# Key and value chunks of a second attention layer moved to the end of a mixture, shorter second tiles, and other loads at the joins, in a two-layer gated Flamingo kernel

## The chip, the cores and the metric

The kernel runs on one NeuronCore of a Trainium2 chip. The metric is the device time of one execution in microseconds (us); lower is better. All arithmetic is in float32; a float32 product shows as two records on TensorE. Engines are named as in the profile: PE is TensorE's matmul, PEld its weight load, DVE VectorE, ACT ScalarE, POOL GpSimd, SP SyncE; PEq, SPq and so on are their sequencers.

## The reference

`x` is 8 x 100 x 512, the context 8 x 722 x 512 with a boolean mask. Four gated steps are added to `x` in turn:

```
x = x + tanh(g_xattn[0]) * L0_xattn(context, layernorm(x), mask)   # 16 heads of 64; queries of x, keys and values of context and x
x = x + tanh(g_ffn[0])   * L0_ffn(layernorm(x))                    # 4 experts, F = 2048, top 2
x = x + tanh(g_xattn[1]) * L1_xattn(layernorm(x), context)         # 16 heads of 32; every 16th context row per head
x = x + tanh(g_ffn[1])   * L1_ffn(layernorm(x))                    # 8 experts, F = 1024, top 2

xattn 0: kv = concat(layernorm(context), layernorm(x)) @ Wkv;  softmax(q k^T, masked) v @ Wout, then layernorm
ffn:     h = silu(x @ w1[e]) * (x @ w3[e]);  out = sum over the 2 chosen experts of gate * (h @ w2[e])
xattn 1: K, V = context @ Wk.T + bk, context @ Wv.T + bv, head h takes rows h, h + 16, h + 32, ...
```

The mask leaves few context rows in use, so that layer 0 works on the gathered valid rows.

## The kernel before, in words

**Prologue.** SP loads the inputs; the masks are scanned into running counts, which POOL writes to DRAM (`cum_d`, L273) and SP broadcasts to all partitions into a part of `wo` (L274 to L277), with half of layer 0's value weights (`wv`) loaded before and after. `few` (L277) is read by every engine, and the branch at L1261 chooses between `attend_to_all` (L631) and `attend_to_few` (L893). The trace takes the second.

**Layer 0's attention** (`attend_to_few`) works on four pairs of batch rows (`Pair`, L942). `find` (L911) turns counts into row numbers, `fetch` (L958) gathers context rows (`ct`). `softmax` (L1074) handles one chunk of two heads for both rows: scores on PE (`ps_sf`), a biased maximum on DVE (L1093), exponentials on ACT (L1103), reciprocal and product on DVE (L1107, L1108). `weigh` (L1113) transposes (`ps_tl`, `ps_tc`) and multiplies by the values (`po_f`). A pair has eight chunks; between them a list `fill` (L1181 to L1257) of steps with costs is worked off in proportion: the next pair's projections, the output projections of the pair before (`project_pair`, L311, its products called `py_w`), and the routing of its rows (`norm_rows`, `route`). The costs only set the place of a step. The fill of the last pair is the output projection and the routing of blocks 4 and 5, the search for the first slot of mixture 0 (`first0.find`, L488 to L565, by generator pieces: DVE's sums, counts `pp_f` on PE, `place` at L541, `pe_f` at L549, then the rows), and two of the four chunks of layer 1's keys and values (`keys_values_1`, L571: per chunk four steps of 16 records; `k1T` and `v1T` written by ACT at L594). The output projection of block 6 is split in two and laid around the last chunk (`project_parts`, L295).

**Mixtures.** `Mixture.run` (L1544) computes slots: up to 256 rows of one expert. `xt` rows are gathered by POOL from the normed rows `xnd` (`fetch`, L1521), transposed (L1563) and copied (`xTs`, L1566), then `pa` and `pb` (L1617), gate (L1625 to L1627) and `py_e` (L1589 or L1600), and added to the accumulator by a scattered DMA (L1659). The first slot of 256 is chosen before all rows are known: from row blocks up to `EARLY0` (6) or `EARLY1`; the rest is planned by `dispatch` (L1281) while it runs. Mixture 0 has a first slot of 256, two of 192 and four of 256; mixture 1 a first of 256, four of 160, three of 128 and two of 256. A slot of 192 or 160 gathers and transposes two tiles of 128 rows, of which the second is used by 64 or 32 rows. `ahead` steps of the deferred work (`late`: project, route) run before the first slot's transposes, the others between its matmuls. Before mixture 0 that is one step, the projection of block 7 (`last_outputs`, L1775). The pools of the attention are released before it, and tiles of the mixture lie where they were.

**Between the mixtures.** `ending` (L1787) loads eight pieces and one weight tile and runs chunks 2 and 3 of layer 1's keys and values (`pkv`, L584) behind the last slot's last product. Then come the row loads (L1809), `normed` (L1824: statistics on DVE, root on POOL, transposes `pt_x`, copies `xT` on ACT), `queries_1` (L1842, `pq`), `set_apart` (L1857, `apartv` on ACT, `apartk` on POOL), `scores_1` and so on, and in the last row blocks the search for mixture 1's first slot (`first1.find`) and the routing. Weights of that slot are loaded early with `begin_weights` (L1539): `w1(0)`, `w3(0)` after the expert is known, `w2(0)` when the index copy `e_late` is written, which is ordered behind the row numbers (L563, L564).

Of the kernel before, what the change touches and what calls it, by code (L numbers as in the profile page):

```python
# [8 lines left out]
FP = mybir.dt.float32  # L9
# [4 lines left out]
ALU = mybir.AluOpType  # L14
# [50 lines left out]
def flamingo_gated(  # L65
# [86 lines left out]
    def load_kv0(pool, tag, i, bufs=1):  # L152

        t = pool.tile([P, KC, 512], FP, tag=tag, name="wkv", bufs=bufs)
        nc.sync.dma_start(t, wkv_r[:, :, bass.ts(i, 512)])
        return t
# [101 lines left out]
    with ExitStack() as ph:  # L258
# [12 lines left out]

        cum0 = wo.rearrange("p c n -> p (c n)")[:, : 2 * CTX]
        wv = [load_kv0(wpool, "wv0", 2)]  # L273
        nc.sync.dma_start(cum0, cum_d[0].partition_broadcast(P))  # L274
        wv.append(load_kv0(wpool, "wv1", 3))
# [19 lines left out]
    def project_parts(b, cuts, ps, tag, work, y_tag="y", y_bufs=1):  # L295

        n = IN0 // P
        py = ps.tile([P, 512], FP, tag=tag, name="py")
        for c in range(n):
            if c in cuts:  # L300
                yield
            nc.tensor.matmul(
                py[:S], oT0[:, c, bass.ts(b % 2, S)], wo[:, c, :], start=(c == 0), stop=(c == n - 1)
            )
        add_normed(b, py, work, y_tag, y_bufs)

    def project_out(b, *where):
        for _ in project_parts(b, (), *where):
            pass
# [165 lines left out]
    class First:  # L475
# [12 lines left out]
        def find(self, space, ps, tag):  # L488
# [58 lines left out]
            for t in range(2):  # L547
                for k in range(b):
                    self.counted = nc.tensor.matmul(  # L549
                        pe[:, bass.ts(t, 2)], place[:, k, bass.ts(t, P)], what[:, k],  # L550
                        start=(k == 0), stop=(k == b - 1),
                    )
# [7 lines left out]
            known = v.scalar_tensor_tensor(  # L560
                self.rows, both[:, :, 0], -1.0, free, ALU.add, ALU.add
            )
            with tc.issue_after(known.ins):  # L563
                v.tensor_copy(self.e_late, number)  # L564
# [43 lines left out]
    def half_square(t, src, h):  # L608
        nc.sync.dma_start(t, src[:, bass.ts(h, D // 2)].rearrange("(c p) n -> p c n", p=P))
        return t  # L610

    def load_heads():
# [4 lines left out]
        def load(c, kc):  # L617
            if kc < 2:
                t = wv[kc]
# [11 lines left out]
    def attend_to_all():  # L631
# [209 lines left out]

        load_x(2, 3)
        wk = [load_kv0(kvp, "wk", i, 2) for i in range(2)]
# [3 lines left out]
        for b in range(B):  # L847
# [24 lines left out]
            if b <= EARLY0:  # L872
                project_out(b, ps_mm, "mm", work, "o", 2)
            if b < EARLY0:
# [4 lines left out]
        for _, step in keys_values_1(  # L879
            (0, 1),  # L880
            lambda: [
                half_square(
                    kvp.tile([P, KC, 512], FP, tag="wk", name="wkv1", bufs=2)[:, :, : D // 2], w, 0
                )
                for w in (wk1, wv1)
            ],
            load_heads(),
# [5 lines left out]
    def attend_to_few():  # L893
# [264 lines left out]
        find(0, cum0)  # L1158
        pair.fetch()
        wk = [load_kv0(kvp, "wk", i, 2) for i in range(2)]  # L1160
# [3 lines left out]
        for k, (_, step) in enumerate(pair.steps()):  # L1164
# [6 lines left out]
            (0, 1),  # L1171
            lambda: [
                half_square(
                    kvp.tile([P, KC, 512], FP, tag="wk", name="wkv1")[:, :, : D // 2], w, 0
                )
                for w in (wk1, wv1)
            ],
            load_heads(),
# [3 lines left out]
        for i in range(PAIRS):  # L1182
# [11 lines left out]
            else:  # L1194
# [3 lines left out]
                c = (0.5, lambda: next(choice, None))  # L1198
                norms, routes = routes
                fill = fill + norms[:1] + kv[:2] + routes[:1] + norms[1:] + kv[2:3] + routes[1:]  # L1200
                fill += [c, kv[3], kv[4], c, c, kv[5], c, kv[6], c, kv[7], c]
# [19 lines left out]
            for c in range(n):  # L1221
                now = softmax(pair, c)
                if following is None and c == n - 1:

                    parts = project_parts(EARLY0, (3, n - 2), ps_mm, "mm", work)
                    fill.insert(-1, (0, lambda: next(parts)))
                while done < len(fill) and (cost < whole * (c + 1) / n or c == n - 1):
# [6 lines left out]
            if following is None:  # L1234
                next(parts)
                finish(*last)
                next(parts, None)
                for _ in choice:
                    pass
                break  # L1240
            finish(*last)
# [258 lines left out]
    class Mixture:  # L1500
# [20 lines left out]
        def fetch(self, rows, k0, T, upto=B):  # L1521

            xts = []
            for k in range(k0, k0 + (T + P - 1) // P):
                xt = ein.tile([P, D], FP, tag="xt", name="xt", bufs=4)
# [4 lines left out]
                    in_offset=bass.IndirectOffsetOnAxis(ap=rows[:, k : k + 1], axis=0),  # L1530
# [13 lines left out]
        def run(self, before, late, ahead, pace, between=None, ending=None):  # L1544
# [13 lines left out]
            def transposed(xts):  # L1558
                xT = ein.tile([P, KC, WHOLE], FP, tag="xTs", name="xTs", bufs=2)
                for t, xt in enumerate(xts):  # L1560
                    pt = ps.tile([P, 512], FP, tag="m", name="pt_s")
                    for kc in range(KC):
                        nc.tensor.transpose(  # L1563
                            pt[:, bass.ts(kc, P)], xt[:, bass.ts(kc, P)], ident
                        )
                    nc.vector.tensor_copy(  # L1566
                        xT[:, :, bass.ts(t, P)], pt.rearrange("p (k s) -> p k s", s=P)
# [133 lines left out]
            def ready():  # L1701
# [3 lines left out]

            xT = slot(
                self.e, self.w0, WHOLE, transposed(self.xts), first.rows, first.gate, 0,
# [67 lines left out]
    def last_outputs(ps, work):  # L1775
        for b in range(EARLY0 + 1, B):
# [10 lines left out]
    def ending(ps):  # L1787

        pieces = [(c, kc) for c in (2, 3) for kc in range(KC)]
        tiles = {}  # L1790
        for c, kc in pieces[:3]:
            t = spaces["heads"].tile([P, 4 * B * M1], FP, name=f"ch{c}{kc}")
            tiles[c, kc] = heads_into(t, c, kc)
        w = wts.tile([P, KC, 512], FP, tag="w1", name="wkv1", bufs=3)
        w = [half_square(w[:, :, bass.ts(i, D // 2)], m, 1) for i, m in enumerate((wk1, wv1))]
        for (c, kc), tag in zip(pieces[3:], ("w3", "w2", "w1", "w3", "w2")):
# [287 lines left out]
```

## Time and profile before

| what | value |
|---|---|
| median of three runs | 1432.19 us (1431.19 to 1440.32) |
| profiled execution: run, span | 1431.09 us, 1429.4 us |
| mean granted PE clock | 0.986 |
| layer 0's attention | about 16 to 409 us |
| mixture 0: first `pa` to last `py_e` | 415.39 to 971.84 us |
| layer 1's attention | about 985 to 1098 us |
| mixture 1: first `pa` to its last `py_e` | 1101.56 to 1413 us |

The profile gives for each engine its busy time and, for idle time in front of an instruction, what ended it. A row of the timeline has start, length, engine, line, operation, output and inputs, count and, in brackets, idle time and its releaser. Waits of a queue's own (SPq) are time in which SP could issue no transfer. The chain of waits follows the last instruction back through its releasers; a row with DMA means that a transfer was what was waited for. The granted clock is 1.00 at full speed; a stretch at half speed shows the same matmuls with double distance from start to start.

### The profile page before, as it was taken

The numbers are of one execution on the slowest core, as the hardware profiler recorded it, in microseconds if no ns is written. First come the engines' busy times: TensorE is split into PE (matmuls) and PEld (weight loads), VectorE is DVE, ScalarE is ACT, GpSimd is POOL, SyncE is SP. The second block draws the span as 40 slices with busy tenths as digits, with TensorE's granted clock in tenths as the row PEclk, the third lists the DMA queues.
The fourth block names the chain that finished last, engine by engine and source line by source line (L and its number), as shares of the span: only waits on it lengthen the run. The fifth ranks groups of instructions, "written<-read, shape, count | busy, mean of one in ns | idle before, by whom it ended". The sixth has DMA issues, their size and how long they took to land. (4 is left out here: it accounts for less than half of the span.)

```text
span 1429.4 us, 18472 instructions
## 1 busy us (share of the span) xinstructions
PE 1362.0 (95%) x7181; PEld 1027.8 (72%) x7181; DVE 485.8 (34%) x1405; ACT 252.3 (18%) x729; POOL 189.4 (13%) x279
## 2 busy tenths in 40 slices
PE   4999999999979999999999999998998999999995
PEld 4566756767557789997777776773666789988773
DVE  4353644535735221212121211113374623223220
ACT  1124423334311000100000000002452101101000
POOL 3410211100130110000010000003321111111000
PEclk9999999999999999999999999998998999999998
DMA  8300101111367365664364535513016478779521
GB/s 296 107 1 0 41 7 34 60 30 48 107 256 293 140 206 214 223 229 135 134 206 167 168 121 190 170 63 84 13 47 226 177 254 284 244 243 344 201 45 17
DMA packets 103892, 208.13 MB, mean 146 GB/s; under 512 B 6198, under 2 KB 13370, under 8 KB 103780
## 3 DMA queue, kind: packets, MB, share of 16 engines
q1 hardware_dynamic: 95556, 186.72, 36.7%
q0 software_dynamic: 8224, 19.97, 5.8%
q8 instruction: 63, 1.03, 0.3%
q14 instruction: 49, 0.40, 0.1%
HBM read 191.45 MB, written 15.23 MB: 145 GB/s over the span
## 5 line engine op out<-in xcount | busy, mean ns | idle before, releaser
L1617 PE MATMUL pa<-xTs,w 128*128 128x256 f32 (+3 forms) x1536 | 314.5, 347 | 1.6 <-DVE xTs L1566 1.6
L1617 PE MATMUL pb<-xTs,w 128*128 128x256 f32 (+3 forms) x1536 | 309.8, 344 | 0.0
L1617 PEld LDWEIGHTS pa<-xTs,w 128*128 128x128 f32 x1536 | 260.2, 191 | 32.7 <-issue 8.9
L1617 PEld LDWEIGHTS pb<-xTs,w 128*128 128x128 f32 x1536 | 260.9, 191 | 21.7
L1600 PE MATMUL py_e<-w,hT 128*128 128x512 f32 x464 | 204.4, 592 | 0.0
L1625 ACT ACTIVATE sg<-pa 128x256 f32<-128x256 f32 (+3 forms) x192 | 66.9, 349 | 692.5 <-PE pa L1617 680.1
L1626 DVE TENSOR_TENSOR sg<-sg,pa 128x256 f32<-128x256 f32 (+3 forms) x192 | 72.3, 377 | 341.9 <-ACT sg L1625 338.8
L1600 PEld LDWEIGHTS py_e<-w,hT 128*128 128x128 f32 x464 | 87.1, 190 | 97.0 <-issue 94.7
L1627 DVE TENSOR_TENSOR hT<-sg,pb 128x256 f32<-128x256 f32 (+3 forms) x192 | 72.3, 377 | 121.2 <-PE pb L1617 119.6
L1065 PE MATMUL pv_f<-wkv,kvT 128*100 128x512 f32 (+1 forms) x192 | 86.2, 597 | 0.0
L1589 PE MATMUL py_e<-hT,w 128*128 128x192 f32 (+1 forms) x512 | 79.0, 313 | 0.0
L1589 PEld LDWEIGHTS py_e<-hT,w 128*128 128x128 f32 x512 | 76.8, 190 | 0.0
L1526 POOL DMA_INDIRECT xt<-xnd,rows x27 | 26.6, 986 | 368.9 <-PE pt_s L1563 277.4
L1051 PE MATMUL pk_f<-kvT,wkv 128*128 128x328 f32 x256 | 73.3, 443 | 1.1 <-ACT kvT L1022 1.0
L1103 ACT ACTIVATE pr_f<-pr_f,nmax 100x228 f32<-100x228 f32 x128 | 60.7, 475 | 35.6 <-DVE nmax L1093 33.4
L1051 PEld LDWEIGHTS pk_f<-kvT,wkv 128*128 128x128 f32 x256 | 47.8, 190 | 24.0 <-ACT kvT L1022 2.1
L1065 PEld LDWEIGHTS pv_f<-wkv,kvT 128*100 128x100 f32 (+1 forms) x192 | 32.6, 174 | 44.1 <-issue 42.0
L1093 DVE CUSTOM_DVE_ANT_0 pr_f<-ps_sf,bias 100x228 f32<-100x228 f32 x128 | 43.7, 391 | 54.5 <-PE ps_sf L1080 54.3
L1659 POOL DMA_INDIRECT xr<-ye,rows x12 | 18.7, 1558 | 267.5 <-DVE ye L1658 266.9
L1035 PE MATMUL pq_f<-kvT,wq 128*128 128x200 f32 x256 | 47.4, 346 | 6.7 <-ACT kvT L1022 3.9
L1035 PEld LDWEIGHTS pq_f<-kvT,wq 128*128 128x128 f32 x256 | 45.4, 198 | 8.0 <-ACT kvT L1022 4.6
L1566 DVE COPY xTs<-pt_s 128x512 f32<-128x512 f32 x31 | 20.3, 687 | 84.9 <-PE pt_s L1563 81.6
(379 smaller groups left out, 1217.9 us busy)
## 6 DMA issues: line engine op xcount, KB each, us to landing
w<-in_f_w_dram SPq DMA_DIRECT2D x144, 1024.0 KB
ch<-in_ctx_heads_dram SPq DMA_DIRECT2D x8, 720.0 KB
wkv<-in_wkv_dram SPq DMA_DIRECT2D x4, 1024.0 KB
wq<-in_ctx_heads_dram SPq DMA_DIRECT2D x4, 720.0 KB
wkv<-in_ctx_heads_dram SPq DMA_DIRECT2D x4, 720.0 KB
kT<-cum_d SPq DMA_DIRECT2D x3, 722.0 KB
wq<-in_wq_dram SPq DMA_DIRECT2D x4, 512.0 KB
wo<-in_wo_dram SPq DMA_DIRECT2D x1, 2048.0 KB
```

The source lines that it names most:

```text
L1035: nc.tensor.matmul(pq[:, bass.ts(i, 2 * S)].rearrange("p (j s) -> p j s", j=2), wq[:, kc, bass.ts(c0 + i, P)], self.lats[kc], start=(kc == 0),
L1051: nc.tensor.matmul(pk[:, : S + FK], wk[c // 4][:, kc, bass.ts(c % 4, P)], self.kvT[:, kc], start=(kc == 0), stop=(kc == KC - 1),)
L1065: nc.tensor.matmul(pv[:n], self.kvT[:, kc, k0 : k0 + n], wv[hf][:, kc, :], start=(kc == 0), stop=(kc == KC - 1),)
L1093: nc.vector.tensor_tensor_reduce(out=pr[:, r, j], in0=ps[:S, r, bass.ts(j, FK)], in1=p.bias[j], scale=-1.0, scalar=FMAX, op0=ALU.add, op1= ...
L1103: nc.scalar.activation(pr[:, r, j], pr[:, r, j], AF.Exp, bias=nmax, scale=-1.0, accum_out=sm[:, r, j : j + 1],)
L1526: nc.gpsimd.indirect_dma_start(out=xt, out_offset=None, in_=xnd[: LEAD + upto * S], in_offset=bass.IndirectOffsetOnAxis(ap=rows[:, k : k + ...
L1589: nc.tensor.matmul(pys[c // 2][:, bass.ts(c % 2, T)], w2[:, i, bass.ts(c, P)], hT[:, i, :T], start=False, stop=(fg == F // FG - 1 and i == ...
L1600: nc.tensor.matmul(py[:n], hT[:, i, c : c + n], w2[:, i, :], start=(fg == 0 and i == 0), stop=(fg == F // FG - 1 and i == FG // P - 1),)
L1617: nc.tensor.matmul(p[:, :T], w[:, kc, bass.ts(i, P)], xT[:, kc, :T], start=(kc == 0), stop=(kc == KC - 1),)
L1625: nc.scalar.activation(sg[:, :T], pa[:, :T], AF.Sigmoid)
L1626: nc.vector.tensor_tensor(sg[:, :T], sg[:, :T], pa[:, :T], ALU.mult)
L1627: nc.vector.tensor_tensor(hT[:, i, :T], sg[:, :T], pb[:, :T], ALU.mult)
```

## The change

Chunk 0 of layer 1's keys and values stays in the last pair; chunks 1, 2 and 3 are computed in `ending`, with 12 pieces instead of eight and the weights in two tiles of 384 columns. Piece 10 and 11 take the places of piece 0 and 1 after the steps that read those. Block 6's output projection is no longer laid around the last chunk; it and block 7's run ahead of the first slot's transposes (`ahead` 2). `find`'s last piece stands directly before the release of the attention's pools. The value weights `wv` and the counts are loaded after the branch, the counts first and into the space of a key weight tile. The second tiles of slots of 192 and 160 are gathered and transposed by their 64 or 32 rows. In layer 1's last row blocks, the ordering of the routing behind `pe_f` is gone, and `w2(0)` of mixture 1 is asked for after the first slot's transposed rows are copied. The core of the diff:

```diff
-        cum0 = wo.rearrange("p c n -> p (c n)")[:, : 2 * CTX]
-        wv = [load_kv0(wpool, "wv0", 2)]
-        nc.sync.dma_start(cum0, cum_d[0].partition_broadcast(P))
-        wv.append(load_kv0(wpool, "wv1", 3))
...
-        find(0, cum0)
+        wk, wv = kv0_tiles(kvp, "wk"), kv0_tiles(kvp, "wv")
+
+        space = bring(0, wk[0])
+        load_kv0(wv, 2)
+        find(0, space)
         pair.fetch()
-        wk = [load_kv0(kvp, "wk", i, 2) for i in range(2)]
+        load_kv0(wk, 0)
         load_x(2, 3)
         load_rest()
...
-            (0, 1),
+            (0,),
             lambda: [
-                half_square(
-                    kvp.tile([P, KC, 512], FP, tag="wk", name="wkv1")[:, :, : D // 2], w, 0
-                )
+                chunks_of(kvp.tile([P, KC, 512], FP, tag="wk", name="wkv1"), w, 0, 1)
...
-                c = (0.5, lambda: next(choice, None))
+                c = (0.2, lambda: next(choice, None))
                 norms, routes = routes
-                fill = fill + norms[:1] + kv[:2] + routes[:1] + norms[1:] + kv[2:3] + routes[1:]
-                fill += [c, kv[3], kv[4], c, c, kv[5], c, kv[6], c, kv[7], c]
+                fill = fill + norms[:1] + routes[:1] + norms[1:] + routes[1:]
+                fill += [c, kv[0], c, c, kv[1], c, kv[2], c]
...
-                if following is None and c == n - 1:
-
-                    parts = project_parts(EARLY0, (3, n - 2), ps_mm, "mm", work)
-                    fill.insert(-1, (0, lambda: next(parts)))
-                while done < len(fill) and (cost < whole * (c + 1) / n or c == n - 1):
+                while done < len(fill) and cost < whole * (c + 1) / n:
...
             if following is None:
-                next(parts)
-                finish(*last)
-                next(parts, None)
+                kv[3][1]()
+            finish(*last)
+            if following is None:
                 for _ in choice:
                     pass
-                break
-            finish(*last)
...
-                xt = ein.tile([P, D], FP, tag="xt", name="xt", bufs=4)
+                n = min(P, T - (k - k0) * P)
+                xt = ein.tile([P, D], FP, tag="xt", name="xt", bufs=4)[:n]
...
+            xT = transposed(self.xts)
+            if len(self.w0) < 3:
+
+                with tc.issue_after(self.copied.ins):
+                    nc.vector.tensor_copy(first.e_late, first.e)
+                self.begin_weights()
...
-        for b in range(EARLY0 + 1, B):
+        for b in range(EARLY0, B):
...
+        for i in range(3):
+            head_piece(i, i)
+        w = [
+            chunks_of(wts.tile([P, KC, 512], FP, tag="w1", name="wkv1", bufs=3), m, 1, 3)
+            for m in (wk1, wv1)
+        ]
+        for i, tag in enumerate(("w1", "w3", "w2", "w3", "w2", "w3")):
+            piece(3 + i, tag)
         yield
+        piece(9, "w2")
...
+        for i, (_, step) in enumerate(steps):
             step()
-
-    mix.run(last_outputs, range(EARLY0, B), 1, 1, between, ending)
+            if i < 2:
+                head_piece(10 + i, i)
+
+    mix.run(last_outputs, range(EARLY0, B), 2, 1, between, ending)
...
-            if b > EARLY1 + 1:
-                xn = norm_rows(b - 1, wk_, out, nc.sync)
-            elif b:
-                logits = route(b - 1, *how)
+            if b:
+                logits = route(
+                    b - 1, ps_t, "t", wk_, wg, lg1, out, nc.scalar.copy, nc.sync
+                )
...
-                with tc.issue_after(first1.counted.ins):
-                    logits = route(b - 1, *how, xn)
-                    project_1(b, oT)
-            else:
-                project_1(b, oT)
+            project_1(b, oT)
...
-        mix.begin_weights()
```

## The prediction

> **What bounds the kernel now.** I read the page's first part, then the busy time by stretch, then, for each stretch in which PE is not full, PE's timeline with what released it, the queue's own waits and the chain. Times are us from the span's start.
>
> ```profile
> PE 1362.0 (95%) x7181; PEld 1027.8 (72%) x7181; DVE 485.8 (34%) x1405; ACT 252.3 (18%) x729; POOL 189.4 (13%) x279
> ```
>
> PE is the bound and nothing else is near. A change can remove PE work, remove PE's idle time, or alter the clock at which PE runs. By stretch (columns: length, then PE, PEld, DVE, ACT, POOL busy, granted clock, DMA share, GB/s):
>
> ```profile
> 341.00:416.00 75.00, 66.28 (x479) 37.84 (x479) 44.69 (x158) 22.57 (x75) 14.61 (x24) 0.98 0.29 104
> 416.00:971.80 555.80, 555.74 (x2496) 442.73 (x2494) 125.92 (x367) 47.68 (x122) 35.57 (x32) 1.00 0.52 182
> 971.80:1001.00 29.20, 22.38 (x170) 11.45 (x170) 10.69 (x25) 8.42 (x19) 12.38 (x27) 0.82 0.31 76
> 1086.00:1101.60 15.60, 13.05 (x49) 8.64 (x49) 4.11 (x12) 0.66 (x2) 3.46 (x5) 0.67 0.92 334
> 1101.60:1413.00 311.40, 311.36 (x1828) 262.47 (x1828) 94.60 (x303) 32.04 (x90) 40.66 (x34) 1.00 0.62 213
> ```
>
> Both mixtures are full. What can be won lies at three joins: into mixture 0, out of it, into mixture 1. The first, on PE's timeline:
>
> ```profile
> 401.74 7.08 PE L302 MATMUL py<-wo,oT 128*100 128x512 f32 x16 [1.88 <-DVE y L362]
> 412.07 0.63 PE L1563 MATMUL pt_s<-ident,xt 128*128 128x128 f32 x4 [3.25 <-issue]
> 413.48 1.12 PE L1563 MATMUL pt_s<-ident,xt 128*128 128x128 f32 x4 [0.78 <-DVE xTs L1566]
> 415.39 1.22 PE L1617 MATMUL pa<-xTs,w 128*128 128x256 f32 x2 [0.80 <-DVE xTs L1566]
> ```
>
> PE waits for the gathered rows. Their numbers were known at 394.7, but POOL and SP stood until row block 6's output norm had left the released pool (DVE L366, done 403.56):
>
> ```profile
> SPq L1276 <- DVE x L366: 14.1, 1, 14.1
> ```
>
> So the gathers went out at 404.43 and 405.84, and the second landed at 412.82. The second join, PE, then ACT:
>
> ```profile
> 971.84 9.89 PE L584 MATMUL pkv<-ch,wkv 128*32 128x360 f32 x128
> 985.42 0.53 PE L1833 MATMUL pt_x<-ident,xn 100*128 100x100 f32 x4 [3.70 <-ACT apartv L1867]
> 991.81 5.60 PE L1845 MATMUL pq<-xT,wq 128*128 128x400 f32 x8 [0.58 <-ACT xT L1836]
> 997.60 2.88 PE L1845 MATMUL pq<-xT,wq 128*128 128x400 f32 x8
> ```
> ```profile
> 983.57 2.90 ACT L1867 COPY apartv<-v1T 32x180 f32<-32x180 f32 x8 [1.22 <-POOL mv L239]
> 986.50 0.49 ACT L1836 COPY xT<-pt_x 128x400 f32<-128x400 f32 x1
> ```
>
> The same eight pq records take 5.60 and 2.88: half clock. The third join is on the chain of waits:
>
> ```profile
> 1084.25 7.26 DMA w<-in_f_w_dram
> 1091.51 1.09 POOL xt L1526
> 1092.91 7.17 DMA xt<-xnd,f_rows
> 1101.56 1.99 PE pa L1617 x8
> ```
>
> **The change part by part.** The sum goes against this execution: span 1429.4, run 1431.09, 1.1 under the median 1432.19.
>
> *1. Prologue.* SP no longer loads wv and the broadcast of the counts before the branch; both follow it. The counts (L274) were issued at 13.29 and landed at 17.67, 4.4 later; issued at 16.1 they land near 20.5, and DVE's search L918 starts there instead of 19.40 (DVE passes its branch only at 19.17): ct's gather is up to 1.1 later. Against that, DVE now takes the first qT copy ahead of ct's statistics, so the last queries no longer wait (2.79 idle before 33.10); values then wait for the second qT copy, which still stands behind ct's normalization (34.64 + 0.57), and start at about 35.3 instead of 35.91. I take -0.6. Bounds: -2 (two thirds of the 2.79) to +3 (SP's branch takes 4.0, as at 965.45, instead of the 0.5 seen at 15.6, and all behind it follows). SP's order after the branch (counts, wv, keys, x, wo) is 2.7 MB ahead of the keys; at the 390 GB/s of these slices this is 7 us, landing near 24, before values ask.
>
> *2. Last pair and first join.* From 340.95 to pa at 415.39 are 74.4; PE's idle times over 0.25 in it add to 8.6, so 65.8 is work. One chunk leaves: four steps at 1.25 to 1.35, 5.2. Row block 6's projection (16 records, 6.9) stays on PE but goes behind the search. Work after: 60.6. Both fillers covered softmax chains of this pair: from the end of a chunk's scores to its transposes are 3.95 (four reduces 1.35, exponentials 1.9 starting 0.45 after the first, reciprocal 0.18, product 1.1). Laying the new order by hand with these rows (scores 1.0, transposes 0.8, weighing 0.85, py_w 5.5), I find stalls of 0.55 before the weighing of chunk 0, 1.85 before block 4's router rows, 1.6 before the search's counts, 0.95 before the weighing of chunk 7, and 3.25 for the search's DVE steps before pe_f: 8.2. The first three would be longer by what DVE has queued. pe_f then ends near 391.4 to 394, against 394.1. Behind it the loads of w (3 MB) and both gathers go out at once, at 392 to 395, since block 6 and 7 no longer lie before the release. Blocks 6 and 7 then hold PE for 13.75, longer than the gather's 7.2, so the 3.25 wait goes; left are two xTs copies, about 2.3. Stalls 10.5 + 60.6 give pa at 412.0; the durations alone, laid end to end, give 409.1, but the same laying puts before's pa 2.6 too early. I take 411, -4.5. Bounds: 409.1 with full clock at pa (before loses 3.3 there: 256-wide records 0.43 apart instead of 0.216 until 420.25), about -10; and half clock over py, below, +9.
>
> *3. Clock at this join.* It was full over py after a gap of 1.88 and half after the three waits that add to 4.8 out of 7 us. After, 5.8 of the 10 us ahead of pe_f are idle, so the half clock probably moves to py, for the 6.7 to 10 us that it lasted at the joins: 3.3 to 5.0 lost there, 3.3 saved at pa. Net 0. Bounds inside the former.
> The Trainium skill, "TensorE: Matmul & The Clock Gate", Part 1, puts half rate behind an idle window of about 3.4 us and full rate after about 3.4 us of steady work. The row differs: at the third join a gap of 1.77 was followed by half clock for 10 us. By the page an estimate of py's loss is 1.7 at most, and the sum would be 1.6 lower, at 1422; the row's longer loss speaks against the change where the page's shorter one speaks for it.
>
> *4. Second join.* Three chunks at the end instead of two: 4.95 more PE (9.89 for two), ending at 986.7. SP's eight early pieces (720 KB each) and two weight loads now stand before mixture 0's last branch, and pieces 9 to 11 behind it; the last waits for step 1 (about 974.5). With the branch of 4.0 the first row block's load goes at about 980.2 instead of 978.88, and DVE and POOL follow by 1.3; this alone gives pq at 993.1. ACT is later still: k1T and v1T to 987.9, 1.2 branch, eight copies 2.9, four xT copies 0.5 each from 992.05: pq at 994.2, +2.4. The chunk's 4.95 is thus half hidden by the wait that was 3.70 and the four short ones. Bounds: +1 (row chain alone) to +7 (load issued at 986, behind the pieces). The clock's loss of 2.7 I leave; gone, the part is -0.3.
>
> *5. Third join.* The copy of e_late, w2(0) and the next group's weights now wait for the transposed rows. So the gathers no longer fly beside 4 MB: 7.17 from issue to landing becomes nearer 3.35 (ct's gather at 59.49, landed 62.84, with the queue quiet): -3.8. Block 6's router rows now come before pe_f and fill part of the 1.77 but wait for xn (1087.4): pe_f ends 0.5 earlier, and 0.8 is lost elsewhere. I take -3.5. Bounds: 0 (gather as slow as 7.17) to -5. The late weights are 4 MB, 10.5 us at 400 GB/s; the first is asked for 13.8 and w2(0) 27 after pa starts, so they are hidden; without cover, 1:1.
>
> *6. Rows alone.* In mixture 0 two second tiles of 64 rows, in mixture 1 four of 32. A full tile's four transposes hold PE for 0.435 (0.87 for two tiles); those of 100 rows stand 0.085 apart against 0.109. In proportion to rows a tile of 64 saves 0.2 and one of 32 saves 0.28, 1.5 together; I take -1.2. Bounds: 0 (copies and transposes cost the same) to -2.6 (all six tiles free). The copies are off the path:
>
> ```profile
> L1566 DVE COPY xTs<-pt_s 128x512 f32<-128x512 f32 x31 | 20.3, 687 | 84.9 <-PE pt_s L1563 81.6 <-DMA w<-in_f_w_dram 3.1
> L1563 PE MATMUL pt_s<-ident,xt 128*128 128x128 f32 x124 | 17.3, 279 | 5.6 <-issue 3.2 <-DMA xt<-xnd,f_rows 1.3 <-DVE xTs L1566 0.8
> ```
>
> *Sum.* -0.6 - 4.5 + 0 + 2.4 - 3.5 - 1.2 = -7.4: 1423.7, and 1424 as a forecast of the median.
>
> **The rivals.** *A, slower: the half clock covers all of py.* Place: blocks 6 and 7, 13.75 of work after 10 us of which 5.8 are idle. At half rate all of it costs 13.75 more: 1424 + 13.75 = 1438. Above 7.4 us of py work at half rate the whole change loses. For it: third join, where 1.77 was enough and the clock stayed low for 10. Against it: no stretch of half clock in this trace lasts over 10 us, which costs 5 and gives 1429 less what pa saves.
> *B: SP's queue decides the second join.* Pieces 10 and 11 stand before the row loads, and if the branch or a slot holds SP until 986, pq comes 12.9 later (978.88 to 991.81), at 999: +7 instead of +2.4, 1429; up to 1434 if the scatter's 4.7 us landing (972.97 to 977.7) is also slowed by the extra 2 MB. Against: the pieces' slots are free early by PE's order.
> *C: nothing visible.* The chunk is paid out in one place and in at another (-5.2 and +4.95), the gather was as slow beside out's write as beside w, and only part 6 remains: 1430.
> *D: every join gains.* Part 1 at -2, part 2 at -10, part 4 at -0.3, part 5 at -5, part 6 at -2.6 is -20: 1411; half of that beyond the sum gives 1414 as its middle. For it: clock lost now is 3.3 + 2.7 + 2.2 at the joins. Against: the last pair has less to fill with.
>
> **How the numbers follow.** Forecast 0.50 (own range 1418 to 1430), A 0.10, B 0.13, C 0.10, D 0.17. The range 1412 to 1438 leaves out the lower half of D, the upper of A and a little that I have not thought of, about 0.17. One per cent is 14.3, about what a measurement of this kernel tells from no change: faster, below 1417.9, has most of D and 0.06 of the forecast, 0.22; slower, above 1446.5, has only unnamed cases and A with B, 0.06; the rest, 0.72, is within.
>
> **What would show it.** Right: pa of mixture 0 near 411 with py ending near 406 and no DMA wait before pt_s; pkv with 192 records ending 14.8 after the last down; pq 2 to 3 later after that down than the 20 of before; at the third join xt landing within 4 of its issue and no w in flight. Wrong: the last pair's stalls over 12; py at 1.7 per pair; xs loads issued after 982; a wait of pa on w in mixture 1's second group, 14 us after its start.

## The result, and the profile after

The changed kernel takes 1436.16 us (median of 12 runs, 1432.65 to 1441.16) against 1433.08 for the kernel before beside it (12 runs, 1428.33 to 1440.32): a ratio of 1.0032, 95% interval 1.0017 to 1.0048. It is slower, by 3.1 us between the two medians and by about 4.6 us by the ratio, 0.2 to 0.3%; the forecast was 1424, a gain. The profiled execution ran 1436.99 us with a span of 1435.3 and a mean clock of 0.979.

Cutting both traces at the same events shows where the two profiled executions differ. Each row is the time between the starts of two kinds of work on PE, in us:

| stretch | before | after | difference |
|---|---|---|---|
| start to the last pair's first `py_w` | 335.34 | 335.09 | -0.25 |
| that to mixture 0's first `pa` | 80.05 | 83.19 | +3.14 |
| mixture 0, to the last `pkv` chunks' start | 556.45 | 554.32 | -2.13 |
| `pkv` start to the first `pq` | 19.97 | 24.40 | +4.43 |
| first to last `pq` | 27.57 | 26.73 | -0.84 |
| last `pq` to mixture 1's first `pa` | 82.18 | 81.82 | -0.36 |
| mixture 1, to PE's last record | 311.75 | 313.85 | +2.10 |

A `pkv` start is also the end of mixture 0's last product, called the last down below.

The page's first part, and the busy time by stretch of the changed kernel (columns as before):

```profile
PE 1368.0 (95%) x7181; PEld 1034.4 (72%) x7181; DVE 482.8 (34%) x1404; ACT 252.2 (18%) x729; POOL 187.8 (13%) x279
```
```profile
341.00:418.20 77.20, 64.94 (x412) 40.59 (x408) 42.84 (x156) 21.52 (x73) 14.97 (x25) 0.87 0.27 97
418.20:972.60 554.40, 554.26 (x2496) 441.36 (x2496) 125.81 (x369) 47.57 (x122) 35.52 (x32) 1.00 0.51 179
972.60:1006.00 33.40, 27.36 (x236) 13.88 (x236) 10.77 (x25) 10.02 (x22) 12.18 (x27) 0.85 0.44 134
1082.00:1105.50 23.50, 19.41 (x100) 11.91 (x96) 12.14 (x46) 2.84 (x9) 6.18 (x8) 0.80 0.41 144
```

PE has as many records as before and is busy 6 us longer. Much of the same work took longer: the granted clock of the last pair and first join fell from 0.98 to 0.87. PE's timeline there:

```profile
366.92 0.93 PE L381 MATMUL pt_r<-ident,xn 100*128 100x100 f32 x4 [2.14 <-DVE xn L245]
367.77 1.84 PE L1071 MATMUL ps_sf<-kT,qT 64*100 64x228 f32 x6
393.08 5.22 PE L543 MATMUL pe_f<-space 100*128 100x2 f32 x24 [3.18 <-DVE space L535]
398.76 16.23 PE L296 MATMUL py<-wo,oT 128*100 128x512 f32 x32 [0.46 <-DVE space L551]
414.82 0.60 PE L1552 MATMUL pt_s<-ident,xt 128*128 128x128 f32 x4
418.28 1.99 PE L1607 MATMUL pa<-xTs,w 128*128 128x256 f32 x8 [1.26 <-DVE xTs L1555]
```

The gathered rows no longer hold PE, as forecast. But the six score records take 1.84 where the same six took 1.01 before, `pe_f` 5.22 instead of 2.74, and the 32 records of blocks 6 and 7 take 16.23 where two times 6.9 were counted. The clock's record in the trace has two half-rate stretches here, 365.8 to 376.0 and 393.1 to 403.4; before it had none in the pair and one at 413.5 to 420.3, in front of `pa`.

The second join, PE, ACT and SP's own waits:

```profile
972.60 14.73 PE L574 MATMUL pkv<-ch,wkv 128*32 128x360 f32 x192
990.90 0.90 PE L1842 MATMUL pt_x<-ident,xn 100*128 100x100 f32 x4 [3.57 <-PEq L1744]
997.00 4.76 PE L1854 MATMUL pq<-xT,wq 128*128 128x400 f32 x8 [0.58 <-ACT xT L1845]
```
```profile
989.25 2.90 ACT L1876 COPY apartv<-v1T 32x180 f32<-32x180 f32 x8 [1.30 <-DMA x<-xr]
992.17 0.49 ACT L1845 COPY xT<-pt_x 128x400 f32<-128x400 f32 x1
```
```profile
SPq L1744 <- SPq L1744: 8.3, 3, 5.5
SPq L1818 <- DMA xr<-ye,rows: 0.2, 1, 0.2
```

ACT is where the forecast put it (first xT copy forecast at 992.05, seen at 992.17). The rows are not: their first load went at 984.81, 12.2 after the last down, where it was 7.0 before. SP was held behind its branch until 0.2 before that, and the scattered rows finished at the same moment (4.7 us after issue before, 9.9 now).

The third join, from the chain of waits:

```profile
1095.38 2.17 PE pe_f L543 x20
1098.41 1.10 POOL xt L1514
1099.82 3.78 DMA xt<-xnd,f_rows
1105.56 3.78 PE pa L1607 x8
```

The gather's flight fell from 7.17 to 3.78, as forecast. But `pe_f` ended 2.6 later after the last `pq` than before. The projections in front of it ran at half clock (1082.6 to 1089.4), and four projection records (1.96) that stood behind it before now run ahead of it; together this took more than the wait of 1.77 that is gone and the full clock of `pe_f` itself (2.17 for 4.39) gave back. And `pa`, 1.99 for eight records before, started at half clock.

### The profile page after: what moved, and what is told of

Its sections match the earlier page's. It is cut to its first block, busy times and chain, and to the rows that moved or that the text cites. A ratio compares the mean times of both kernels' runs of the same rounds, so it can differ in the third digit from the quotient of the medians.

```text
span 1435.3 us, 18479 instructions
## 1 busy us (share of the span) xinstructions
PE 1368.0 (95%) x7181; PEld 1034.4 (72%) x7181; DVE 482.8 (34%) x1404; ACT 252.2 (18%) x729; POOL 187.8 (13%) x279
## 5 line engine op out<-in xcount | busy, mean ns | idle before, releaser
L1555 DVE COPY xTs<-pt_s 128x512 f32<-128x512 f32 (+2 forms) x31 | 18.1, 618 | 83.1 <-PE pt_s L1552 83.1
```

## The experiments

All stretches below are read from one profiled execution each, in the cuts of the table: P for the last pair and first join (80.05 before, 83.19 changed), J for `pkv` to `pq` (19.97, 24.40), T for last `pq` to mixture 1's `pa` (82.18, 81.82).

**e1, two chunks in the pair again.**

```diff
-            (0,),
+            (0, 1),
...
-                fill = fill + norms[:1] + routes[:1] + norms[1:] + routes[1:]
-                fill += [c, kv[0], c, c, kv[1], c, kv[2], c]
+                fill = fill + norms[:1] + kv[:2] + routes[:1] + norms[1:] + kv[2:3] + routes[1:]
+                fill += [c, kv[3], kv[4], c, c, kv[5], c, kv[6], c]
...
-        chunks = (1, 2, 3)
+        chunks = (2, 3)
```

> The changed kernel with chunks 0 and 1 in the last pair again and 2 and 3 at the end; all else as changed. Theory T (clock and SP's queue): the emptied last pair fell to half clock from 367 to 377, and SP's late pieces held the row loads. Then the first loss and the second join's go: the stretch 367 to 377 is at full clock, mixture 0's first pa starts at 412 to 415 instead of 418.3, and from the last down's end to pq it is 20 again instead of 24.4; 5 to 9 us below the changed kernel, so about 1428 where that is 1436. Rival R1 (the chunk is only shifted, and the loss lies in the order of the joins): pa later by 5 of the chunk, the end earlier by 5, and within 1.5 us of the changed kernel.

1434.05 us, ratio to before 1.0001 (0.9979 to 1.0024): by the two ratios 4.4 below the changed kernel, not the 5 to 9 expected. The end behaved as expected: J is 18.95, and the row loads go 7.03 after the last down. The pair did not: P is 87.31, 4.1 more than the changed kernel, with half clock at 378.4 to 388.7 and 398.9 to 409.1. The chunk alone does not keep the pair full. Block 6's projection, 6.9 of work, is missing there too. So the theory had to be widened to all the work taken out of the pair.

**e2, the wait ahead of `pe_f` filled.**

```diff
+                t = ps_mm.tile([P, 512], FP, tag="mm", name="warm")
+                for k in range(4):
+                    nc.tensor.matmul(
+                        t[:S], oT0[:, k % 8, bass.ts(0, S)], wo[:, k % 8, :],
+                        start=True, stop=True,
+                    )
                 for _ in choice:
                     pass
```

> The changed kernel with four extra products of the output projection (512 columns each, 0.86 us each at full clock, results unused) ahead of pe_f, three of them in the wait of 3.2 us there. Theory T: it is the wait that drops the clock; with it filled, pe_f takes 2.7 instead of 5.2 and the 16 py products 13.75 instead of 16.2, and mixture 0's first pa comes about 4 earlier (5 less some 0.9 for the fourth product). Rival R2 (the half clock comes from the whole thin stretch from 356 on, in which PE idles and transposes, or from no fixed cause): pe_f and py stay at 5.2 and 16.2 and pa is 0 to 1 later.

1435.53 us, 1.0015 (0.9994 to 1.0035). P is 79.85, 3.3 less (about 4 were expected), although work was added. PE's timeline:

```profile
390.92 2.82 PE L1229 MATMUL warm<-wo,oT 128*100 128x512 f32 x6
394.01 2.81 PE L543 MATMUL pe_f<-space 100*128 100x2 f32 x24 [0.27 <-DVE space L535]
397.28 15.60 PE L296 MATMUL py<-wo,oT 128*100 128x512 f32 x32 [0.46 <-DVE space L551]
416.18 1.99 PE L1613 MATMUL pa<-xTs,w 128*128 128x256 f32 x8 [1.25 <-DVE xTs L1561]
```

`pe_f` is at full speed again. The second stretch of half clock shrank from 10.2 to 3.4 us (397.2 to 400.6) but did not go; the first, at 366.5, is untouched, as nothing was put there. So the wait ahead of `pe_f` was paid twice in the changed kernel: as a wait, and as half clock behind it.

**e3, the last two pieces from ACT's queue; e4, without them; e10, without the last three.** The diffs of e3 and e10 (e4 is the second part of e10's alone). In e4 and e10 the steps of the pieces that are left out multiply pieces already there:

```diff
-                head_piece(10 + i, i)
+                head_piece(10 + i, i, nc.scalar)
```
```diff
-        piece(9, "w2")
+        tiles[pieces[9]] = tiles[pieces[3]]
...
-                head_piece(10 + i, i)
+                tiles[pieces[10 + i]] = tiles[pieces[i]]
```

> The changed kernel with the last two pieces of the heads (10 and 11) issued by ACT's queue instead of SP's; the same bytes at the same time. Theory T-queue (SP stands before them, and its branch of 5.5 us comes after): SP passes the branch some 4 us earlier; if that alone held the row loads they go at 979 to 981 instead of 984.8 and pq comes 2.5 earlier (then ACT's copies end last). Theory T-scatter (the pieces' bytes delay the scattered rows, landing 9.9 after issue instead of 4.7): row loads stay at about 984.8 behind the scatter, and the time is that of the changed kernel.

> The changed kernel without loading pieces 10 and 11: steps 10 and 11 multiply pieces 0 and 1 again, so part of chunk 3's keys and values is wrong by intention and its load is left out. Both forms of theory T: row loads go at 979 to 980.5 and the scattered rows land about 5 after their issue; pq then waits for ACT's copies and comes at 994 to 995 instead of 997.0, 2 to 3 us less in all. Rival R1 (the second join is late only since PE ends 5 later): pq stays at 997.

> The changed kernel without loading pieces 9, 10 and 11: their steps multiply pieces 3, 0 and 1, so part of chunk 3's keys and values is not computed from its own data, the routing behind it differs, and only the second join is read. Theory T-scatter: with no piece behind the last slot, the last scatter lands 4.7 after its issue as before (9.9 changed, 7.0 without the last two), the row loads go 7.1 to 8 after the last down (12.2 changed), and pq waits for ACT's copies alone: 22 to 22.6 after the last down, the +2.4 of the forecast. Rival: landing stays above 6.5 or pq at 24.

e3: 1438.41 us, 1.0042 (1.0017 to 1.0067), not better. SP reaches its branch 2.6 earlier after the last down (0.5 against 3.1), yet J is 24.61. e4's time (1489.8) is that of another routing, with one more slot behind mixture 1, and says nothing; e10's one time likewise. Their second joins, side by side:

| | scatter, issue to end | SP, branch to first wait for rows | row load after last down | J |
|---|---|---|---|---|
| before | 4.7 | 6.6 | 7.0 | 19.97 |
| changed | 9.9 | 9.0 | 12.2 | 24.40 |
| e3 | 10.1 | 11.4 | 12.4 | 24.61 |
| e4 | 7.0 | 6.9 | 9.3 | 22.83 |
| e10 | 4.7 | 5.3 | 7.1 | 22.30 |

SP's waits in e10, in the stretch of that join:

```profile
SPq L1818 <- DMA xr<-ye,rows: 8.1, 1, 8.1
SPq L595 <- PE py_e L1590: 6.5, 1, 6.5
SPq L1744 <- SPq L1744: 4.6, 1, 4.6
```

With the bytes gone SP is through its branch early and waits 8.1 for the scatter, as before's 6.8; `pq` then waits for ACT alone, at +2.3 where 2.4 was forecast. With the bytes there, issued by whom ever, the scatter takes 5.2 longer than before and SP's way 2.4 (changed) or 4.8 (e3) longer, and SP then waits only 0.2 or 0.5 for the scatter. The trace tells what SP does on that way. From the branch to its first semaphore wait are 4.0 us before, 5.6 in the changed kernel and 5.1 in e3; behind that, in the changed kernel and e3, it waits for the landing of the pieces, also of those that ACT issued: until 983.79 for the piece that landed at 983.78 in the changed kernel, until 977.33, 980.05 and 982.75 in e3, where the three pieces landed at 977.31, 980.04 and 982.74. So it is the pieces' 2.2 MB in flight that count, whichever queue issues them: they slow the scatter, and SP waits for them as well. In all five the scatter is what SP waited for last; in the changed kernel and e3 a faster scatter alone would have gained no more than the 0.2 or 0.5. The one piece left in e4 costs the scatter 2.3, the two further ones 2.9.

**e5, pair and end as before; e6, only the split projection back; e7, all the pair's waits filled.** e5 takes the pair's code, `project_parts` and `ending` from the kernel before; its core is the first diff. e6 and e7 are shown against the changed kernel; e7 has e2's four products ahead of `pe_f` as well:

```diff
-                fill = fill + norms[:1] + routes[:1] + norms[1:] + routes[1:]
-                fill += [c, kv[0], c, c, kv[1], c, kv[2], c]
+                fill = fill + norms[:1] + kv[:2] + routes[:1] + norms[1:] + kv[2:3] + routes[1:]
+                fill += [c, kv[3], kv[4], c, c, kv[5], c, kv[6], c, kv[7], c]
...
-        chunks = (1, 2, 3)
+        chunks = (2, 3)
...
-    mix.run(last_outputs, range(EARLY0, B), 2, 1, between, ending)
+    mix.run(last_outputs, range(EARLY0, B), 1, 1, between, ending)
```

```diff
-                fill = fill + norms[:1] + routes[:1] + norms[1:] + routes[1:]
-                fill += [c, kv[0], c, c, kv[1], c, kv[2], c]
+                fill = fill + norms[:1] + kv[:1] + routes[:1] + norms[1:] + kv[1:2] + routes[1:]
+                fill += [c, kv[2], c, c, kv[3], c, c, c]
...
+                    parts = project_parts(EARLY0, (3, n - 2), ps_mm, "mm", work)
+                    fill.insert(-1, (0, lambda: next(parts)))
```

```diff
+                def more():
+                    t = ps_mm.tile([P, 512], FP, tag="mm", name="warm")
+                    for k in range(2):
+                        nc.tensor.matmul(
+                            t[:S], wo[:, k, : S], wo[:, k, :], start=True, stop=True
+                        )
...
+                fill = fill + norms[:1] + w + w + routes[:1] + norms[1:] + w + routes[1:]
```

> The changed kernel with the last pair, block 6's split projection and the end of mixture 0 as before (two chunks in the pair, two at the end); what stays of the change are the prologue, the second tiles by rows alone and the third join. Theory T: both losses sit in what is undone here, so the last pair runs at full clock and mixture 0's first pa follows the pair's first output products by 80 as before (83.2 changed), pq follows the last down by 20 (24.4 changed), and the gain of the third join and of the rows stays: 3 to 5 below the kernel before, about 1427 where before is 1431.5. Rival R3 (the loss sits in the third join or the prologue): not faster than before.

> The changed kernel with block 6's projection split around the last chunk again and the one chunk's steps spread early in the pair; three chunks still at the end. Theory T as sharpened by the first runs (it is all the work taken out of the pair, chunk and projection, that leaves PE thin enough for the half clock): with the projection's 6.9 back in the pair, one of the two stretches of half clock goes, and pa follows the pair's first output products by 75 to 79 instead of 83.2 (5 below the 80 of before is the chunk, if no clock is lost). Rival R4 (the chunk alone decides): both stretches stay and it is 82 or more. The second join stays late, 24 from last down to pq.

> The changed kernel with extra products (512 columns, results unused) in the pair's waits: six early in the pair beside the four ahead of pe_f. Theory T: no stretch of half clock between 340 and 420; py and pe_f at full clock, and although 5 to 8 us of useless work is added, pa follows the pair's first output products by 78 to 82 instead of 83.2. Rival R2 (no link between filled waits and clock): half clock stays and pa is later by the added work, 86 to 90.

e5: 1432.97 us, 1.0011 (0.9996 to 1.0026). Both losses are gone (P 79.61, J 19.79) and T is 80.03, 2.2 less than before; but mixture 1 takes 313.44 against 311.75, because the half clock now lies in its first slot. It does not beat the kernel before: this expectation failed in its last step. e6: 1434.82, 1.0023 (1.0002 to 1.0044); P is 80.90, between the two expectations, with 10.2 us of half clock at 378.5 and two stretches of 3.4. e7: 1432.97, 1.0006 (0.9988 to 1.0025); half clock between 340 and 420 falls from 20.5 us to 10.2, where none was expected, and P is 79.52: 3.7 shorter than the changed kernel with ten useless products of 0.86 more. The busy time by stretch, changed and then e7:

```profile
355.00:366.00 11.00, 6.25 (x62) 4.12 (x60) 10.45 (x32) 6.17 (x23) 3.20 (x8) 0.99 0.08 23
366.00:377.00 11.00, 10.09 (x52) 6.45 (x52) 6.11 (x20) 3.08 (x12) 4.85 (x7) 0.54 0.17 53
```
```profile
355.00:366.00 11.00, 9.12 (x68) 5.00 (x65) 10.05 (x32) 5.16 (x19) 3.79 (x9) 1.00 0.13 39
366.00:377.00 11.00, 11.00 (x78) 6.68 (x80) 7.44 (x24) 3.98 (x14) 4.20 (x6) 0.84 0.12 37
```

In the changed kernel PE was busy 6.25 of the first 11 us, with eight waits of which none is longer than 2.14, and the next 11 ran at 0.54; in e7, with 9.12, they ran at 0.84. Since the two kernels differ in the added products alone, it is the thin stretch that brings the half clock on, shown in one execution each.

But the busy share alone does not say when. Half clock begins and ends on steps of 3.4 us (from 365.8 to 393.1, where the two stretches of the changed kernel begin, are eight). Here are such steps with what came behind them, in the kernel before and in e7:

```profile
399.85:403.26 3.41, 1.53 (x5) 0.75 (x5) 3.08 (x4) 0.00 (x0) 2.03 (x3) 1.00 0.00 0
403.26:406.67 3.41, 3.41 (x9) 1.33 (x8) 0.31 (x1) 0.00 (x0) 1.94 (x2) 1.00 0.46 112
```
```profile
391.76:395.17 3.41, 3.41 (x25) 2.66 (x23) 0.62 (x1) 0.00 (x0) 0.00 (x0) 1.00 0.00 0
395.17:402.00 6.83, 6.22 (x11) 2.75 (x12) 0.52 (x4) 0.00 (x0) 4.38 (x6) 0.50 0.62 199
```

Before, PE was busy 1.53 of 3.41 us with 512 columns wide `py`, and full clock followed. In e7 it was busy throughout, for the most part with `pe_f`'s records of two columns, and half clock followed. So what PE does in a stretch matters beside how long it is busy. The thin stretch of the last pair also holds many transposes; no run here varied those, and e11 below is the only one that varies the narrow records.

**e8, the late weights early again.**

```diff
+            with tc.issue_after(known.ins):
+                v.tensor_copy(self.e_late, number)
...
+        mix.begin_weights()
     spaces["xn"].release()
```

> The changed kernel with the late index copy and the loads of w2 and the next group right behind the rows' numbers again, as before. If the third join's change works as forecast, the gather flies beside 4 MB again and takes 6.5 to 7.5 instead of 3.8, and mixture 1's first pa comes 2.5 to 3.5 later after its gather's issue than in the changed kernel; the time is 2 to 3 above it. Rival R5 (the gather is not slowed by those loads): its flight stays under 4.5 and pa does not move.

1442.86 us, 1.0074 (1.0056 to 1.0093); by the two ratios some 6 above the changed kernel, where 2 to 3 were expected. The chain:

```profile
1104.32 7.14 DMA xt<-xnd,f_rows
1111.50 1.13 PE pt_s L1556 x4
1113.40 3.78 PE pa L1611 x8
```

The flight is 7.14 again, and from the gather's issue to `pa` are 9.1 instead of 5.7. T is 85.16, 3.3 more. Most of the rest of this execution lies in the pair, whose code is that of the changed kernel: its first half-rate stretch is 17.1 us long instead of 10.2, and P is 85.95, 2.8 more.

**e11, wide products between `pe_f`'s narrow ones.**

```diff
                         pe[:, bass.ts(t, 2)], place[:, k, bass.ts(t, P)], what[:, k],
                         start=(k == 0), stop=(k == b - 1),
                     )
+                    if E == E0:
+                        nc.tensor.matmul(
+                            wide[:, :P], ident, ident, start=True, stop=True
+                        )
```

> Kernel e2 (extra products ahead of pe_f) with one 128-column product between each two of pe_f's 2-column products (1.3 us more work, unused). e2 still had half clock for 3.4 right behind pe_f, although PE waited for only 0.7 there. Theory N (narrow products do not count as work for the clock): that stretch goes, py is at full clock throughout, and pa comes within 0.5 of e2's place although 1.3 is added. Rival R2: the stretch stays, and pa is 1 to 1.5 later.

1437.76 us, 1.0042 (1.0026 to 1.0058). There is no half clock between 379 and 990 in its trace, where e2 had 3.4 us behind `pe_f`. But early in the pair there were 13.6 us of half clock, in two stretches, instead of 10.2, and P is 81.23, 1.4 over e2: against the expectation in place, for it in clock. One execution each; I take it as a hint.

**e9 and e12, the waits of the three joins filled in e5.** e12 differs from e9 in its counts alone (12, 4, 2 and 3 instead of 26, 12, 5 to 6 and 6, none behind the last `pkv`):

```diff
+            def keep(t, n):
+                for k in range(n):
+                    nc.tensor.matmul(
+                        t[:, bass.ts(k % 4, P)], ident, ident, start=True, stop=True
+                    )
...
+                    keep(pt, idle[t])
...
+                        if w0 and not fg and not i:
+                            keep(pa, 2)
...
-            xT = transposed(self.xts)
+            xT = transposed(self.xts, (12 if E == E0 else 4, 2))
...
+            for k in range(3 if 0 < b < B // 2 else 0):
+                nc.tensor.matmul(
+                    pt[:, 1, bass.ts(k % 4, P)], ident, ident, start=True, stop=True
+                )
```

> Kernel e5 (last pair and end as before, the rest as changed) with extra 128-column products (results unused, about 0.11 each) in the waits of the three joins: 26 ahead of the first transposes of mixture 0, 30 behind the last pkv, 6 ahead of the transposes of row blocks 1 to 3, 12 ahead of mixture 1's first transposes, 5 and 6 in the two short waits behind. Theory T (waits cost twice, once as such and again by the half clock after them): no half clock at the three joins; 2.1, 2.7 and 1.7 less in the first pa, pq and mixture 1's pa, so 5 to 7 below e5 and before, about 1426 where before is 1432. Rival R2 (no link): half clock stays and the time is that of e5 or up to 1 above it.

> Kernel e9 with fewer extra products, since each took 0.23 and not 0.11, so that 26 and 30 of them outlasted the waits they were to fill: 12 ahead of mixture 0's first transposes, 4 ahead of mixture 1's, 2 in each short wait behind, 3 ahead of row blocks 1 to 3, none behind the last pkv (they pushed PE's branch of 3.3 back). Theory T: mixture 0's first pa runs at full clock (2.1 less than e5's stretch from pa to pkv, 556.7 to 554.5) with no delay of pa, mixture 1's likewise 0.5 to 1.7 less; the second join, where PE's own branch leaves it idle, keeps half clock; 2 to 4 below e5 and before, 1429 to 1431 where before is 1432.5. Rival: half clock only moves to another stretch and the time is that of e5.

e9: 1440.1 us, 1.0045 (1.0026 to 1.0065). A product took 0.23, twice my count, so that the fillers outlasted the waits: `pt_s` began at 418.02 behind 52 filler records, and PE's branch behind 60 others. e12: 1428.15 us against 1432.30 beside it, 0.9969 (0.9946 to 0.9991), below both kernels, and below e5 (1.0011, 0.9996 to 1.0026), from which it differs by the extra products alone. Its clock is 0.991, and the stretches of the joins are at 1.00, 0.94 and 1.00:

```profile
341.00:416.00 75.00, 70.54 (x522) 42.45 (x520) 45.29 (x159) 22.57 (x75) 16.61 (x28) 1.00 0.27 96
971.80:1001.00 29.20, 25.09 (x192) 15.35 (x185) 10.04 (x24) 9.98 (x22) 14.39 (x29) 0.94 0.27 71
1086.00:1101.60 15.60, 14.22 (x94) 11.99 (x95) 5.27 (x16) 2.98 (x6) 4.26 (x6) 1.00 0.61 194
```

The second join, which I had not expected to gain, did: its 16 `pq` records take 5.61, where eight took 5.60 before.

## Why the prediction was wrong

The forecast failed in its sign: -7.4 was forecast, and the two profiled executions differ by +6.1 at PE's last record. By the table, parts 2 and 3 together came to +1.0 (3.14 - 2.13) where -4.5 was forecast, part 4 to +3.6 (4.43 - 0.84) where +2.4 was forecast, and parts 5 and 6 to about +1.7 (2.10 - 0.36) where -4.7 was forecast. So the first and the third join carry most of the miss, and at both it is mostly the clock, which the sum had at 0. By its parts:

1. Prologue, -0.6: it was -1.9 at the first scores (75.70 to 73.80) and -0.25 by the last pair, after 3.4 us of half clock at 79.1. With the same prologue the last pair is reached 1.3 to 1.6 earlier than before in the three traces that have no half clock up to there (e3, e6, e10), and 1.0 to 2.3 later in those that have 3.4 to 6.8 us of it between 33 and 42. So without half clock there the part gained more than was forecast; why it falls there in some traces stays open.
2. Last pair and first join, -4.5: the wait for gathered rows is gone, as forecast. Of the listed stalls two came near their size (2.14 for 1.85, 3.18 for 3.25), and the 1.6 before the search's counts did not come. But up to the stall of 2.14 the list had one of 0.55, where seven from 0.22 to 0.90 add to 3.5; these make the thin stretch. By durations `pa` was laid at 409.1; without the clock's loss it would have come at 418.28 - 9.7 = 408.6, an estimate from the two losses under 3.
3. Clock, 0: this is the step that failed first. The forecast moved one stretch, 3.3 to 5.0 lost and 3.3 saved. There were two. The first, from 365.8, was not seen at all: the stalls of 0.5 to 2 us in the pair were listed as costs of their own, without asking what they do to the clock. It cost 4.7 (by the same records' lengths), the second 5.0 (2.5 in `pe_f`, 2.5 in py). What was saved at `pa` was 2.1, not 3.3. e2 and e7 show that filling the waits brings 3.3 and 3.7 back, in spite of the work added; e8 shows the pair's code, unchanged, 2.8 slower with a longer stretch. Rival A named the place and not the size: it put the bound at 13.75.
4. Second join, +2.4: it was +4.4 at the first `pq`. The mechanism of rival B decided, in its second form: the scatter slowed by the added bytes, which the forecast named as an aside worth up to 1434. The term of the sum, ACT's chain, is right: +2.3 in e10. The scatter that all rows wait for was priced at its old 4.7 while 2.2 MB were put beside it; the third join of the same trace showed what 4 MB do to a gather (7.17). SP's branch was taken at 4.0; it took 9.0 with the wait for the pieces' landing, which the forecast had not.
5. Third join, -3.5: the gather's part is right (3.35 forecast, 3.78 seen; 7.14 when undone). The sum failed on the clock here too, and on `pe_f`, which was to end 0.5 earlier and ended 2.6 later. In the traces without added products at this join where no half clock fell into 1080 to 1090, T is 78.97 to 79.67, 2.5 to 3.2 below before; in the changed kernel's profile it fell there, and T gained 0.36. But in every one of these traces half clock then reached into mixture 1's first slot, which cost 1.5 to 2.1 (mixture 1 takes 313.2 to 313.9 where 311.75 was before, the traces with another routing left out). Of T's gain 0.7 to 1.6 is left after that in e1, e2 and e7; in the changed kernel a loss of 1.7 remains.
6. Rows alone, -1.2: nothing. Eight transposes of a full and a short tile hold PE for 0.89 to 0.92, those of two full tiles 0.87. By the form of the groups:

```profile
L1552 PE MATMUL pt_s<-ident,xt 128*128 128x128 f32 x100 | 14.6, 280 | 4.0 <-DMA xt<-xnd,f_rows 3.1 <-DVE xTs L1555 0.9
L1552 PE MATMUL pt_s<-ident,xt 32*128 32x32 f32 x16 | 1.7, 227 | 0.0
L1552 PEld LDWEIGHTS pt_s<-ident,xt 32*128 32x128 f32 x16 | 1.3, 136 | 0.7 <-issue 0.7
```

   Short transposes, once under way, do follow each other closer: 0.062 from start to start for 32 or 64 rows, where full ones stand 0.109 apart. But at the change of shape this is lost: the first short one comes 0.203 behind the last full one, the second 0.08 to 0.11 behind the first, and the next product 0.15 behind the last short one, where 0.109 was usual. The weight load of 136 ns is still 128 columns wide. The scaling by rows came from two shapes, 0.085 for 100 rows and 0.109 for 128, that each stood among their own kind; the change between shapes was put at nothing. The lower bound, 0, was right.

On the rule cited there, from the Trainium skill, "TensorE: Matmul & The Clock Gate", Part 1: the runs agree with it in the step, for every half-rate stretch here, but for the last of each trace, which the end of the record cuts, is a multiple of 3.4 us long (3.4, 6.8, 10.2, 13.7, 17.1). They differ from its table in what sets it off: in the changed kernel's pair only the second stretch followed a wait near that length, 3.18; the first followed a run of waits of 0.2 to 2.14, and in e7 half clock followed 3.4 us without a wait. The measurement decides.

## What to carry to other kernels

On an engine that is busy 95% of the time, count a wait twice: as itself, and as the half clock that a thin stretch brings behind it. Before moving filler work out of a chain of short dependent steps, add up PE's busy share of the 11 us or so there; 0.57 cost the next 10 us half their speed here, 0.83 a third of that. Look also at what the busy time consists of: 3.4 us filled mostly with records of two columns were followed by half clock as well. Before moving transfers, list what lands at the same time with a waiter: a scatter or gather that took 4.7 or 3.8 without them took 9.9 or 7.1 beside 2 to 4 MB.

## What the runs showed of the hardware that was not expected

- Half clock can follow waits that are all short, and its length varies with the same code: the first stretch in the same last pair was 10.2 us long in four kernels and 17.1 in a fifth, which made the pair 2.8 us longer. The spread between runs of one kernel goes with the clock too: of the changed kernel's twelve the fastest, 1432.65 us, had a mean clock of 0.983, the slowest, 1441.16, of 0.977.
- Useless products in the waits made a kernel faster: 0.9969 (0.9946 to 0.9991) of before in e12, 1.0011 (0.9996 to 1.0026) without them in e5.
- SP's way through its branch, 5.3 us in e10 and 6.6 before, took 9.0 and 11.4 with the pieces in flight, since behind the branch SP waited until they had landed, even those that ACT's queue had issued (e3).
- A float32 product of 128 columns took 0.23 us and a transpose of the same shape 0.109; transposes of 32 or 64 rows stood 0.062 apart, but the first behind a full one came 0.203 after it.
